# Macaron block with a state-space layer: B, C and dt in one projection, B stored four states side by side, clip and all products on GpSimd, new places in the order

## The chip, the cores and the metric

The kernel runs on one core of a Trainium2 chip. A core has five engines that run side by side and meet at semaphores: PE (TensorE, matmuls; PEld is its loading of weights), DVE (VectorE), ACT (ScalarE), POOL (GpSimd) and SP (SyncE, which issues nearly all DMAs here). The metric is the device time of one execution in microseconds; lower is better. The profile is one execution, read by a hardware profiler; an engine's "busy" time is the time in which at least one of its instructions ran.

## What is computed

The input x has 32 batches of 512 positions with 256 features. Three layers follow each other, each on the result of the one before: a feed-forward layer at half weight, a state-space layer, and the same feed-forward layer again.

```python
x = x + 0.5 * ffn(layernorm(x))
x = x + ssm(layernorm(x))
x = x + 0.5 * ffn(layernorm(x))
# ffn: every matmul's inputs are rounded to a grid of FP4 values in blocks of 16
h = silu(fp4(x) @ fp4(w_gate).T) * (fp4(x) @ fp4(w_up).T)      # 256 -> 704
y = fp4(h) @ fp4(w_down).T                                      # 704 -> 256
# ssm: N = 16 states for each of 256 features, R = 64
BC = x @ W_in + b_in;  B, C = BC[..., :16], BC[..., 16:]
dt = clip(softplus((x @ W_dt1 + b_dt1) @ W_dt2 + b_dt2), 1e-7, 1e6)
tmp = A * dt
h[t] = exp(tmp) * h[t-1] + expm1(tmp) / tmp * dt * B * x        # along the 512 positions
y = sum(h * C, over the states) + D * x
```

## The kernel before

**Order.** The kernel does not issue instructions where its loops stand. Its loops hand operations to a planner (`Plan.op`): engine, name, what is read, what is written. Each operation has a place in time, a number in the table `WHEN` under its name plus `PERIOD` for every batch. `Plan.run` then takes, again and again, among the operations whose inputs are ready and whose buffers are free in the plan, the one with the lowest number, and issues it. So the table sets the order on every engine's queue, the DMA queue of SP included; the hardware then runs each queue in that order and waits where it has to. The table is the same for all 32 batches. In the result several batches are under way at once: a batch's state-space layer runs beside feed-forward layers of its neighbours.

**Feed-forward** (`ffn`, L664). Layer norm (sums on DVE, four tiny operations on POOL, scaling on ACT), rounding to the grid (`quantize`, L527: the block's top, scale, reciprocal and quotient on DVE into the PSUM buffer `q`, square and curve on ACT, two matmuls with a large diagonal on PE that do the rounding, L563, a copy out on ACT, L569, and the product with the scale on POOL, L570), transposes on PE. Then four tiles of 128 positions: the "gate" and "up" matmuls (L676) in two halves of 352 columns, silu on ACT (L686), a copy of "up" on ACT (L696) and the product of both on POOL (L699); rounding; transposes (L710), copies (L715), the "down" matmuls (L722) and the sum (L729). One tile is different: in `(0, 0)`, the first tile of the first feed-forward layer, DVE multiplies straight out of PSUM (L692, "up silu") and neither the copy nor POOL's product is made.

**State-space layer** (`ssm`, L733). After layer norm and transposes, PE projects to B and C (L743, 32 columns) and, apart from that, to dt's 64 inner columns (L750). ACT adds the two biases (L745, L752). The 32 rows of B and C go to DRAM (L748). PE makes dt's 256 features in two halves (L757), ACT takes softplus (L761) in PSUM, DVE clips into SBUF (L764). Then for each half of the features (c) and each pair of states (NG = 2), 16 pairs in all: two rows of B and two of C come back from DRAM, spread to all 128 partitions (L780, L782, 512 KB each, two buffers each); ACT makes exp and tanh (L789, L792); POOL multiplies x with B, a pair at a time (L796); DVE makes, for each state, two products (L803, L806) and the scan along the positions (L809); POOL multiplies with C (L812); PE adds the states up while it turns them back (L818). A table load on ACT goes before each change between the function groups of silu, softplus and exp with tanh.

**Buffers.** PSUM: three of `pt` (projections, gates, transposes), one `q`, two `eb` (tanh to scan), one `py`.

Of the kernel before, what the change touches and what calls it, by code (L numbers as in the profile page):

```python
# [9 lines left out]
F32 = mybir.dt.float32  # L10
BF16 = mybir.dt.bfloat16
AF = mybir.ActivationFunctionType
# [19 lines left out]
        "weights load": (7249, 7248, 7249, 7249, 6726, 6726, 6642, 6642, 6642, 6841, 6841, 6841,  # L32
        6841),
        "weights x top": (7249, 7065, 7353),
        "weights x scale": (7250, 7248, 7385),
        "weights x rinv": (7250, 7248, 7391),
        "weights x quotient": (7250, 7248, 7391),
        "weights x square": (7250, 7249, 7392),
        "weights x curve": (7250, 7249, 7392),
        "weights x grid": (7250, 7249, 7557),  # L40
        "weights x rounded": (7250, 7249, 7557),
        "weights x value": (7250, 7249, 7558),
        "weights turn": (7251, 7251, 7249, 7249, 7558, 7558),
        "weights turned": (7251, 7251, 7250, 7251, 7558, 7558),
        "weights load down": (7065, 6579),
        "weights h top": (7558, 6642),
        "weights h scale": (7571, 6642),
        "weights h rinv": (7571, 6642),
        "weights h quotient": (7571, 6643),
        "weights h square": (7590, 6643),  # L50
        "weights h curve": (7590, 6643),
        "weights h grid": (7590, 6643),
        "weights h rounded": (7590, 6643),
        "weights h value": (7795, 7065),
        "weights turn down": (7795, 7795, 7699, 7661),
        "weights turned down": (7897, 7814, 8179, 7699),
        "weights zero rows": (8077, 8345),
        "in load": (0,),
        "ffn 0 stats": (1267, 1773, 601, 2361),
        "ffn 0 mean": (1913, 2355, 1536, 3584),  # L60
        "ffn 0 var + eps": (4038,),
        "ffn 0 rstd": (4045,),
        "ffn 0 - mean": (3609,),
        "ffn 0 shift": (4249,),
        "ffn 0 normal": (4499, 5056, 6579, 4467),
        "ffn 0 x top": (6643,),
        "ffn 0 x scale": (6726,),
        "ffn 0 x rinv": (6822,),
        "ffn 0 x quotient": (6835,),
        "ffn 0 x square": (6841,),  # L70
        "ffn 0 x curve": (6873,),
# [815 lines left out]
```

## Time and profile before

| | us |
|---|---|
| median of three runs | 3604.99 (3603.73 to 3605.07) |
| profiled execution, its own time | 3604.13 |
| profiled execution, span on the core | 3602.2 |
| DVE busy | 3409.9 |
| ACT busy | 3385.7 |
| PE busy | 3348.0 |
| POOL busy | 3332.3 |

The engines' shares are close to each other, so the page's totals alone do not say which of them sets the time. The stretch from the start to the first scan, the long repeating middle, and the stretch after the last scan have to be read apart, and in the middle the waits tell more than the busy shares. Numbers such as L796 are lines of the kernel file; "x512" is how often an instruction ran; after the bar stand the busy time, the mean of one, the idle time just before, and what ended it. DMA share is the mean busy share of 16 DMA engines.

### The profile page before, as it was taken

The page shows a single profiled execution, that of the slowest core. Times are in us where ns is not written, and L with a number is a line of the kernel's source. Part 1 is how long each engine was busy: PE and PEld are TensorE (multiplying, and loading weights), DVE is VectorE, ACT ScalarE, POOL GpSimd, SP SyncE. Part 2 cuts the span into 40 slices and gives each one's busy share as a digit, 9 for nine tenths or more (in the row PEclk, how much of TensorE's full clock was granted, in tenths as well). Part 3 has the DMA queues.
Part 4 walks back from the last instruction along what each step waited for, and adds up shares of the span by engine and source line. Part 5 has one row for each costly group of instructions (what it writes and reads, how often), then busy time and mean ns, then how long its engine had stood idle before and what let it go on. Part 6 is the DMA issues. An engine that isn't in the chain of part 4 may idle for free. (4 is left out here: it accounts for less than half of the span.)

```text
span 3602.2 us, 51333 instructions
## 1 busy us (share of the span) xinstructions
PE 3348.0 (93%) x16604; PEld 2443.6 (68%) x16826; DVE 3409.9 (95%) x5280; ACT 3385.7 (94%) x5813; POOL 3332.3 (93%) x1963
## 2 busy tenths in 40 slices
PE   5779999999999999999999999999999999999966
PEld 3457777667767767777766776776777776777654
DVE  3699999999999999999999999999999999999992
ACT  4689999999999999999999999999999999999973
POOL 2589999999999999999999999999999999999992
PEclk9899999999999999999999999999999999999988
DMA  1354545444545545454544454444555454445440
GB/s 45 112 173 166 173 164 176 165 169 165 176 171 170 165 158 175 170 173 164 177 165 169 165 176 170 170 165 159 176 171 173 163 177 165 168 161 169 171 170 12
DMA packets 186652, 578.36 MB, mean 161 GB/s; under 512 B 19664, under 2 KB 54032, under 8 KB 186384
## 3 DMA queue, kind: packets, MB, share of 16 engines
q1 hardware_dynamic: 184816, 574.89, 46.7%
q8 instruction: 133, 2.18, 0.2%
q14 instruction: 135, 1.11, 0.1%
q10 hardware_dynamic: 1568, 0.18, 0.0%
HBM read 556.12 MB, written 18.87 MB: 160 GB/s over the span
## 5 line engine op out<-in xcount | busy, mean ns | idle before, releaser
L676 PE MATMUL pt<-w_guT,xqT 128*128 128x352 f32 x4096 | 1317.4, 466 | 26.1 <-DVE dt L764 16.3
L812 POOL TENSOR_TENSOR hs<-hs,bc 128x1024 f32<-128x1024 f32 x512 | 1214.0, 2371 | 9.3 <-DVE hs L809 2.6
L809 DVE TENSOR_TENSOR_SCAN hs<-ab,eb 128x512 f32<-128x512 f32 x1024 | 1202.4, 1197 | 4.5
L796 POOL TENSOR_TENSOR bx<-xT,bc 128x1024 f32<-128x1024 f32 x512 | 1171.2, 2294 | 30.3 <-DVE eb L806 15.9
L676 PEld LDWEIGHTS pt<-w_guT,xqT 128*128 128x128 f32 x4096 | 753.3, 192 | 409.7 <-DVE dt L764 24.0
L792 ACT ACTIVATE eb<-dt,a_half 128x512 f32<-128x512 f32 x1024 | 708.1, 700 | 36.1 <-DVE hs L809 29.5
L806 DVE SCALAR_TENSOR_TENSOR eb<-eb,a_inv,bx 128x512 f32<-128x512 f32 x1024 | 734.9, 743 | 2.7
L722 PE MATMUL pt<-w_dT,hqT 128*128 128x256 f32 x3072 | 717.0, 383 | 14.8 <-ACT hqT L715 14.8
L789 ACT ACTIVATE ab<-dt,a_sb 128x512 f32<-128x512 f32 x1024 | 700.8, 727 | 1.5
L803 DVE SCALAR_TENSOR_TENSOR eb<-ab,eb 128x512 f32<-128x512 f32 x1024 | 684.5, 682 | 11.4 <-ACT eb L792 7.6
L722 PEld LDWEIGHTS pt<-w_dT,hqT 128*128 128x128 f32 x3072 | 580.1, 192 | 140.4 <-ACT hqT L715 32.9
L818 PE MATMUL py<-ident,hs 128*128 128x128 f32 x4096 | 536.1, 276 | 26.1 <-POOL hs L812 25.8
L818 PEld LDWEIGHTS py<-ident,hs 128*128 128x128 f32 x4096 | 469.4, 142 | 102.0 <-POOL hs L812 38.3
L570 POOL TENSOR_TENSOR h_q<-h_q,h_sc 128x704 f32<-128x704 f32 x258 | 360.3, 1397 | 53.2 <-ACT h_q L569 52.6
L699 POOL TENSOR_TENSOR h<-h,sl 128x704 f32<-128x704 f32 x224 | 379.0, 1692 | 27.4 <-ACT h L696 22.4
L544 DVE TENSOR_REDUCE q<-h 128x44 f32<-128x704 f32 x258 | 227.0, 880 | 68.6 <-POOL h L699 43.8
L710 PE MATMUL pt<-ident,h_q 128*128 128x128 f32 x1536 | 237.0, 278 | 41.2 <-ACT h L696 24.1
L563 PE MATMUL q<-h_m,eye 128*128 128x192 bf16 (+1 forms) x873 | 191.6, 305 | 70.9 <-ACT h_m L556 62.0
L710 PEld LDWEIGHTS pt<-ident,h_q 128*128 128x128 f32 x1536 | 180.5, 141 | 110.3 <-ACT h L696 51.8
L563 PEld LDWEIGHTS <-eye 128*128 128x128 bf16 x1300 | 125.2, 99 | 183.9 <-issue 106.8
L715 ACT COPY hqT<-pt 128x256 f32<-128x256 f32 (+1 forms) x512 | 233.9, 487 | 6.1 <-PE pt L710 5.7
L686 ACT ACTIVATE sl<-pt 128x352 f32<-128x352 f32 x512 | 222.5, 463 | 16.6 <-PE pt L676 13.8
(78 smaller groups left out, 4134.6 us busy)
## 6 DMA issues: line engine op xcount, KB each, us to landing
bc<-rows SPq DMA_DIRECT2D x1024, 512.0 KB, 4.1
x<-in_L_attn_x_dram SPq DMA_DIRECT2D x32, 512.0 KB, 5.2
out_dram<-x SPq DMA_DIRECT2D x32, 512.0 KB, 7.3
rows<-bc SPq DMA_DIRECT2D x32, 64.0 KB, 3.4
xn<-in_L_ffn_w_up_dram SPq DMA_DIRECT2D x6, 128.0 KB, 2.2
h<-in_L_ffn_w_down_dram SPq DMA_DIRECT2D x2, 352.0 KB, 3.4
xn<-in_L_ffn_w_gate_dram SPq DMA_DIRECT2D x5, 128.0 KB, 2.2
w_dt_sb<-in_L_attn_W_dt_dram ACTq DMA_DIRECT2D x2, 64.0 KB, 5.5
```

What stands on the lines that cost most here:

```text
L676: pe.matmul(to()[:, :HALF], lhsT=xqT()[:, c, j * P : (j + 1) * P], rhs=w_guT()[:, c, o : o + HALF], start=(c == 0), stop=(c == NC - 1),)
L699: op("POOL", "product", lambda sl=sl, h=h: g.tensor_tensor(h(), h(), sl(), ALU.mult), [h, sl], [h])
L710: pe.transpose(pt()[:, i * P : (i + 1) * P], hq()[:, kcol[k] : kcol[k] + P], ident)
L722: pe.matmul(po()[:, :DM], lhsT=hqT()[:, k, :], rhs=w_dT()[:, k, :], start=(k == 0), stop=False,)
L789: op("ACT", "exp", lambda c=c, i=i, k=k, ab=ab: s.activation(ab()[:, i, :], dt()[:, c, :], AF.Exp, scale=a_sb[:, c, k : k + 1]), [(dt, c)] ...
L792: op("ACT", "tanh", lambda c=c, i=i, k=k, eb=eb: s.activation(eb[i](), dt()[:, c, :], AF.Tanh, scale=a_half[:, c, k : k + 1]), [(dt, c)], ...
L796: op("POOL", "x b", lambda c=c, bx=bx, bn=bn: g.tensor_tensor(bx().rearrange("p n l -> p l n"), xT()[:, c, :].unsqueeze(2).to_broadcast([P ...
L803: op("DVE", "e", lambda i=i, ab=ab, eb=eb: v.scalar_tensor_tensor(eb[i](), ab()[:, i, :], 1.0, eb[i](), ALU.add, ALU.mult), [(ab, i), eb[i ...
L806: op("DVE", "e x b", lambda c=c, i=i, k=n + i, eb=eb, bx=bx: v.scalar_tensor_tensor(eb[i](), eb[i](), a_inv[:, c, k : k + 1], bx()[:, i, : ...
L809: op("DVE", "scan", lambda i=i, h=h, ab=ab, eb=eb: v.tensor_tensor_scan(h()[:, i, :], ab()[:, i, :], eb[i](), 0.0, ALU.mult, ALU.add), [(a ...
L812: op("POOL", "h c", lambda h=h, cn=cn: g.tensor_tensor(flat(h()), flat(h()), flat(cn()), ALU.mult), [h, cn], [h])
L818: pe.matmul(py()[:, j, :], lhsT=h()[:, i, j * P : (j + 1) * P], rhs=ident, is_transpose=True, start=False, stop=False, skip_group_check=True,)
```

## The change

- **One projection.** The weights of dt's inner columns, B and C stand side by side in one tile of 96 columns (`w_p_sb`); one projection and one bias instruction take the place of two. dt's second matmul reads rows 0 to 63 of the result.
- **B is turned.** PE transposes B's 16 rows (four transposes of 128 positions), ACT copies the result, and four DMAs write it to DRAM so that the four states of a group (XG = 4) stand side by side for each position. C's rows are written as before.
- **x times B by fours.** B is loaded for four states at once, 1 MB, and POOL's product runs over 256 positions by four states: as many instructions of as many elements, with B read in runs of four and x spread over four instead of two. The result is written as before with the positions of a state side by side. Two instructions make a group's four states, one for each half of the positions.
- **Clip on POOL.** Softplus writes SBUF, POOL clips in place.
- **All products on POOL.** Tile (0, 0) loses its special form: ACT copies "up", POOL multiplies.
- **Places.** `WHEN` has new numbers throughout, and the first, second, last but one and last batch have tables of their own. The output is stored in four pieces of 128 KB, each behind its tile, instead of one of 512 KB.

The diff, without the tables:

```diff
-    def __init__(self):
-        self.ops, self.slots = [], {}
+    def __init__(self, tables):
+        self.ops, self.slots, self.tables = [], {}, tables
...
-        o.at = (WHEN[o.name][k] + self.batch * PERIOD, len(self.ops))
+        table = self.tables.get(self.batch, WHEN)
+        o.at = (table[o.name][k] + self.batch * PERIOD, len(self.ops))
...
+    XG = 4
...
-    nc.scalar.dma_start(w_in_sb, w_in.rearrange("(c p) n -> p c n", p=P))
-    nc.scalar.dma_start(w_dt1_sb, w_dt1.rearrange("(c p) r -> p c r", p=P))
+    nc.scalar.dma_start(w_p_sb[:, :, R:], w_in.rearrange("(c p) n -> p c n", p=P))
+    nc.scalar.dma_start(w_p_sb[:, :, :R], w_dt1.rearrange("(c p) r -> p c r", p=P))
...
-    plan = Plan()
+    plan = Plan({0: FIRST, 1: SECOND, NB - 2: LAST_BUT_ONE, NB - 1: LAST})
...
-                if (which, j) in BY_DVE:
+                if (which, j) in PRODUCT_BY_DVE:
...
-        op("PE", "bc", lambda: project(pbc()[: 2 * N, :], w_in_sb), [xT], [pbc])
-        bc = new(sp, [2 * N, L], F32, "bc", 1)
-        op("ACT", "bc bias", lambda: s.activation(
-            bc(), pbc()[: 2 * N, :], AF.Identity, bias=b_in_sb), [pbc], [bc])
-        rows = new(dr, [2 * N, L], F32, "rows", 2)
-        op("SP", "rows", lambda: nc.sync.dma_start(rows(), bc()), [bc], [rows])
-        p1 = new(ps, [P, L], F32, "pt", PT)
-        op("PE", "dt1", lambda: project(p1()[:R, :], w_dt1_sb), [xT], [p1])
-        r1 = new(sp, [R, L], F32, "r1", 1)
-        op("ACT", "dt1 bias", lambda: s.activation(
-            r1(), p1()[:R, :], AF.Identity, bias=b_dt1_sb), [p1], [r1])
+        op("PE", "project", project, [xT], [pbc])
+        bc = new(sp, [R + 2 * N, L], F32, "bc", 1)
+        op("ACT", "project bias", lambda: s.activation(
+            bc(), pbc()[: R + 2 * N, :], AF.Identity, bias=b_p_sb), [pbc], [bc])
+        rows_c = new(dr, [N, L], F32, "rows_c", 2)
+        op("SP", "rows c", lambda: nc.sync.dma_start(rows_c(), bc()[R + N :, :]), [bc], [rows_c])
+        pb = new(ps, [P, L], F32, "pt", PT)
+
+        def turn_b():
+            for j in range(NJ):
+                pe.transpose(pb()[:, j * N : (j + 1) * N], bc()[R : R + N, j * P : (j + 1) * P],
+                             ident[R : R + N, R : R + N])
+
+        op("PE", "turn b", turn_b, [bc], [pb])
+        bT = new(sp, [P, NJ, N], F32, "bT", 2)
+        op("ACT", "turned b", lambda: s.copy(flat(bT()), pb()[:, : NJ * N]), [pb], [bT])
+        rows_b = new(dr, [N // XG, L, XG], F32, "rows_b", 2)
+
+        def side_by_side():
+            with nc.allow_non_contiguous_dma(reason="the states of a group side by side, 32 KB"):
+                for i in range(N // XG):
+                    nc.sync.dma_start(
+                        rows_b()[i].rearrange("(j p) n -> p j n", p=P),
+                        bT()[:, :, i * XG : (i + 1) * XG])
+
+        op("SP", "rows b", side_by_side, [bT], [rows_b])
...
-            op("DVE", "dt", lambda c=c: v.tensor_scalar(
-                dt()[:, c, :], p2[c](), 1e-7, 1e6, ALU.max, ALU.min), [p2[c]], [(dt, c)])
+            if CLIP_BY == "POOL":
+                op("ACT", "softplus", lambda c=c: s.activation(
+                    dt()[:, c, :], p2[c](), AF.Softplus, bias=b_dt2_sb[:, c : c + 1]),
+                   p2[c:], [(dt, c)])
+                op("POOL", "dt", lambda c=c: g.tensor_scalar(
+                    dt()[:, c, :], dt()[:, c, :], 1e6, 1e-7, ALU.min, ALU.max),
+                   [(dt, c)], [(dt, c)])
...
-                bn, cn = (new(st, [P, NG, L], F32, f"bc{i}", 2) for i in range(2))
-                op("SP", "load b", lambda n=n, bn=bn: nc.sync.dma_start(
-                    bn(), rows()[n : n + NG, :].partition_broadcast(P)), [rows], [bn])
+                if n % XG == 0:
+                    bn = new(st, [P, L, XG], F32, "bn", 2)
+                    bx = new(st, [P, XG, L], F32, "bx", 2)
+                    op("SP", "load b", lambda n=n, bn=bn: nc.sync.dma_start(
+                        bn(), rows_b()[n // XG].partition_broadcast(P)), [rows_b], [bn])
+                    for o in range(0, L, L * NG // XG):
+                        t = slice(o, o + L * NG // XG)
+                        op("POOL", "x b", lambda c=c, bx=bx, bn=bn, t=t: g.tensor_tensor(
+                            bx()[:, :, t].rearrange("p n l -> p l n"),
+                            xT()[:, c, t].unsqueeze(2).to_broadcast([P, L * NG // XG, XG]),
+                            bn()[:, t, :], ALU.mult), [(xT, c), bn], [(bx, o)])
+                cn = new(st, [P, NG, L], F32, "cn", 2)
...
-                bx = new(st, [P, NG, L], F32, "bx", 2)
-                op("POOL", "x b", lambda c=c, bx=bx, bn=bn: g.tensor_tensor(
-                    bx().rearrange("p n l -> p l n"),
-                    xT()[:, c, :].unsqueeze(2).to_broadcast([P, L, NG]),
-                    bn().rearrange("p n l -> p l n"), ALU.mult),
-                   [(xT, c), bn], [bx])
...
-        op("SP", "store", lambda b=b, x3=x3: nc.sync.dma_start(
-            out[b].rearrange("(j p) d -> p j d", p=P), x3()), [x3], [])
+        for j in range(NJ):
+            op("SP", "store", lambda b=b, j=j, x3=x3: nc.sync.dma_start(
+                out[b, j * P : (j + 1) * P, :], x3()[:, j, :]), [(x3, j)], [])
```

## The prediction

> **What bounds the kernel now.** I read the page's first part, the busy time in stretches, the waits in the repeating middle, the groups of instructions and the DMA issues, in that order. Overall, then in stretches (columns: stretch, its length, busy time and instruction count of PE, PEld, DVE, ACT, POOL, then PE's clock, DMA share, GB/s):
>
> ```profile
> PE 3348.0 (93%) x16604; PEld 2443.6 (68%) x16826; DVE 3409.9 (95%) x5280; ACT 3385.7 (94%) x5813; POOL 3332.3 (93%) x1963
> ```
>
> ```profile
> 0.00:132.00 132.00, 80.91 (x282) 48.90 (x286) 42.28 (x94) 63.77 (x100) 32.72 (x38) 0.92 0.16 50
> 132.00:200.00 68.00, 47.95 (x222) 36.07 (x223) 66.14 (x100) 53.73 (x91) 59.79 (x29) 0.85 0.50 174
> 200.00:300.00 100.00, 87.03 (x414) 61.45 (x418) 96.25 (x149) 91.74 (x153) 92.04 (x55) 0.97 0.48 164
> 300.00:3300.00 3000.00, 2896.90 (x14588) 2125.19 (x14784) 2981.89 (x4615) 2959.18 (x5105) 2927.00 (x1722) 1.00 0.49 169
> ...
> 3400.00:3517.50 117.50, 81.97 (x393) 59.86 (x397) 110.77 (x152) 89.10 (x144) 104.48 (x54) 0.84 0.48 166
> 3517.50:3602.20 84.70, 56.01 (x217) 39.01 (x217) 14.88 (x29) 30.82 (x55) 19.17 (x15) 0.84 0.04 13
> ```
>
> From 300 to 3300 us DVE is busy 99.4%, ACT 98.6%, POOL 97.6%, PE 96.6%. The run loses its time in the first 132 us (before the first scan) and the last 85 (after the last one). The middle repeats exactly: the one DMA per batch that writes the rows of B and C (timeline of SP) goes out at
>
> ```profile
> 1068.48 0.42 SPq L748 DMA_DIRECT2D rows<-bc  x1
> ...
> 2877.46 0.42 SPq L748 DMA_DIRECT2D rows<-bc  x1
> ```
>
> 17 batches apart, so (2877.46 - 1068.48) / 17 = 106.41 us a batch. Waits between 1000 and 2000 us: DVE has none at all, ACT these:
>
> ```profile
> ACT x L729 <- PE pt L726: 2.6, 9, 0.3
> ACT xn_s L522 <- POOL shift L519: 1.9, 9, 0.2
> ACT eb L792 <- DVE hs L809: 1.8, 9, 0.2
> ```
>
> That is 6.3 us in 1000, 0.67 us a batch. So DVE is the bound and ACT is second by only 0.67 us: without waits it would need 106.41 - 0.67 = 105.74 us. This decides the case: taking work off DVE is worth at most what ACT lets through.
>
> The rows that price the change:
>
> ```profile
> L796 POOL TENSOR_TENSOR bx<-xT,bc 128x1024 f32<-128x1024 f32 x512 | 1171.2, 2294 | 30.3 <-DVE eb L806 15.9
> L699 POOL TENSOR_TENSOR h<-h,sl 128x704 f32<-128x704 f32 x224 | 379.0, 1692 | 27.4 <-ACT h L696 22.4 <-issue 2.7 <-DVE h_sc L546 1.6
> L570 POOL TENSOR_TENSOR h_q<-h_q,h_sc 128x704 f32<-128x704 f32 x258 | 360.3, 1397 | 53.2 <-ACT h_q L569 52.6 <-DVE eb L806 0.4
> L570 POOL TENSOR_TENSOR x_q<-x_q,x_sc 128x1024 f32<-128x1024 f32 x67 | 129.7, 1936 | 60.5 <-ACT x_q L569 60.5
> L692 DVE TENSOR_TENSOR h<-pt,sl 128x352 f32<-128x352 f32 x64 | 32.8, 512 | 13.3 <-PE pt L676 10.2
> L764 DVE TENSOR_SCALAR dt<-pt 128x512 f32<-128x512 f32 x64 | 40.4, 671 | 14.9 <-ACT pt L761 14.9
> L696 ACT COPY h<-pt 128x352 f32<-128x352 f32 x448 | 191.2, 450 | 7.9 <-PE pt L676 7.6
> L745 ACT ACTIVATE bc<-pt,b_in_sb 32x512 f32<-32x512 f32 x32 | 21.2, 664 | 1.2 <-PE pt L741 1.2
> ```
>
> ```profile
> bc<-rows SPq DMA_DIRECT2D x1024, 512.0 KB, 4.1
> out_dram<-x SPq DMA_DIRECT2D x32, 512.0 KB, 7.3
> rows<-bc SPq DMA_DIRECT2D x32, 64.0 KB, 3.4
> d_sb<-in_L_attn_D_dram ACTq DMA_DIRECT2D x1, 1.0 KB, 2.1
> ```
>
> **DVE** loses the product of tile 0 (32.8 us) and the clip (40.4): -73.2, or 2.3 us a batch; its floor falls to 104.1.
>
> **ACT** gains 64 copies of "up" at 191.2 / 448 = 0.427: +27.3. Two bias instructions become one (rows of 512 elements whatever the partitions): -21.2. One new copy per batch of 64 elements: the copies of 512 and 256 elements take 596 and 378 ns, so 64 come to 215: +6.8. Softplus writes SBUF instead of PSUM; exp (to SBUF, 727 ns) against tanh (to PSUM, 700) gives 0 to +1.7, I take +0.9. Table loads by the new order: 286 against 284, at 1.283: +2.6, none of it in the middle (9 a batch in both). Sum +16.4; in the middle 0.43 a batch, so ACT's floor becomes 105.74 + 0.43 = 106.17. ACT is the new bound, and the repeating middle can gain only 0.24 us a batch.
>
> **POOL** gains 32 products at 1.692: +54.1. The 64 clips (512 elements, in place) are not in the trace. Above: the two value rows give (1936 - 1397) / 320 = 1.68 ns an element, so 1.07 us. Below: GpSimd's memsets of 1 and 128 elements (98 and 204 ns) extrapolate to 0.53. I take the middle, 0.80, as a clip lies between them (one read, one write): +51 (34 to 69). The x-times-B product keeps its count (512 of 1024 elements) but now spreads each x over four products, reads B in runs of four, and writes with the old stride. Below: the value product, whose second input is spread over 16, 1936 ns. Above: 2294, no gain; I exclude a loss, since the writes are strided as before and the reads less so. I take 2.05, nearer the value row: -125 (0 to -183). The clip waits on POOL for softplus, and behind it stand an h-times-C and the batch's first x-times-B; DVE, which waited there before, had one wait of note, 14.9 us in the head. POOL in all 3332.3 + 54.1 + 51 - 125 = 3312 (3237 to 3455): its load hardly changes, 0.6 us a batch less.
>
> [...]
>
> **PE** loses one of two projections (60.9 us for the 32-column one) and gains 128 transposes of 16 columns, between 0.1 us (a weight load alone, 109 ns) and 0.28 (a transpose of 128): +13 to +35. All beside other work.
>
> **DMA and SP.** B comes in 256 loads of 1 MB for 512 of 512 KB, the same bytes. New are four small DMAs a batch, 512 pieces of 16 bytes each, between the turned B and the first load of B. Let X be their time to landing, all four. Below: 2.1 us (the D vector, 256 pieces of 4 bytes). Above: the output store, 512 pieces of 1 KB, 7.3, then three more at 5.2: 22.9. I take 8: as many pieces as the store, 1/64 of its bytes. What hides X: in the new order ACT runs 19.3 us of work (by the rows' durations, softplus and three table loads included) from the turned B to the first exp of that batch, and about 4 us more pass to the first e-times-B on DVE: 23. The chain beside it: four issues at 0.35, X, a 1 MB load (4.1 for half; 6), two halves of x-times-B (4.2): 11.6 + X. So it is covered up to X = 11.4. Queued on SP behind the wait for the turned B are one piece of the output, one load of C for the batch before, and the first two loads of B; POOL waits for them. [...]
>
> **Places.** ACT idles 216.5 us before: 68.2 up to 132 us, 22.5 up to 300, 40.8 + 2.7 up to 3400, 28.4 up to 3517.5, and 53.9 after.
> - Middle: 19.5 us of the idle are waits, the rest gaps of some nanoseconds between instructions. Behind a DVE that is now 2 us ahead I take two thirds of the waits away: -13 (0 to -19.5; new waits are a rival).
> - 132 to 300 and 3400 to 3517.5: DVE is busy 273.2 of 285.5 us, it bounds there, and 2.1% of its work is gone: -6.
> - Head: the bias of B and C is reached after the same instructions of PE as before, in another order: the last matmuls of "gate" and "up" now stand before tile 2's rounding, where four used to stand after it. In DVE's timeline the tops of the four tiles start at 62.7, 69.3, 78.5 and 91.5 us, and one weight block waits 10.3 us at 46: against an even 6.6 a tile that is 2.6 + 6.4 + 10.3, some 19 us that an order could save; I take 12. The longer path of B (X - 3.4, a longer load, a second half of the product: about 9) is partly covered by 18 "gate" and "up" matmuls of the next batch moved beside it; I take 4. So -8 (from +9 to -19).
> - Tail: after the last scan stand the same four tiles in both; the last copy ends 3.9 us before the end, and the store behind it shrinks from 512 to 128 KB: -2. Order within: -2 (+5 to -6).
>
> **Sum**, against the profiled execution: 3602.2 + 16.4 - 13 - 6 - 8 - 4 = 3587.6, plus 1.9 around the span (3604.13 - 3602.2) = 3589.5. The median of the runs is 0.9 above that execution: 3590.
>
> **Rivals.**
> 1. POOL becomes the bound: slower. POOL needs 103.8 us a batch now, plus about 0.6 of gaps. It decides when 103.8 + 1.7 + 1.6 - 16 d exceeds 105.6, d being what one x-times-B gains: from d under 0.095 us, a product above 2.20 us. With no gain and the dear clip, 107.6 + 0.6 = 108.2 a batch: +1.8 x 31 = 56, about 3650 with the rest of the sum. For it: the strided writes stay. Against: both rows with a widely spread input are below 2 ns an element.
> 2. The small DMAs land late: X above 11.4 stalls POOL, then DVE, then ACT once a batch. X = 13 gives 1.6 x 31 = +50: 3640. For it: 2048 pieces a batch. Against: the D vector's 2.1 us.
> 3. The new order couples worse: with buffers as few (two for e, one for q, three for pt), ACT waits up to 1 us a batch more rather than 0.42 less: up to 1.42 x 31 = 44, 3605 to 3634. For it: ACT and POOL share more hand-overs (product, clip) than DVE did. Against: ACT's waits of 0.67 are few though it is within 0.7% of the bound already.
> 4. Better than forecast: no waits of ACT in the middle, all 19 us of the head: 3602.2 + 16.4 - 19.5 - 6 - 19 - 6 + 2.8 = 3571.
>
> **How the numbers follow.** Forecast 0.45 (its own range 3574 to 3605: 0.36 faster, 0.09 about the same); rival 4 0.17; rival 3 0.16 (0.07 same, 0.09 slower); rival 1 0.10; rival 2 0.12. 0.2% is 7.2 us, about what a measurement of this kernel can tell from no change. Faster 0.53, same 0.16, slower 0.31. The range takes rival 4 and most of 3, and reaches to the near ends of 1 and 2: 3562 to 3640.
>
> **What would show it.** Right: ACT 99% or more of the middle with waits near nothing, DVE near 98%; the period 106.1 to 106.4; x-times-B near 2.05 us; the clip near 0.8. Wrong: POOL waiting for the loads of B once a batch (rival 2), POOL's share of the middle above 99% (rival 1), ACT's waits above 1 us a batch (rival 3), a first scan later than 136 us (the head).

## The result: slower by 0.9%, and the profile after

The changed kernel takes 3635.33 us, median of four runs (3633.61 to 3643.2), against 3604.82 before: a ratio of 1.0089, 95% interval [1.0072, 1.0107]. The profiled execution took 3633.61 us with a span of 3631.8, 29.6 us longer than the span before.

The first line of the page after, and the busy time in stretches (columns as in the prediction):

```profile
PE 3337.3 (92%) x16605; PEld 2463.0 (68%) x16826; DVE 3405.7 (94%) x5152; ACT 3415.4 (94%) x5879; POOL 3294.1 (91%) x2059
```

```profile
0.00:132.00 132.00, 88.87 (x325) 55.80 (x330) 55.48 (x110) 80.51 (x131) 48.74 (x48) 0.95 0.23 67
...
300.00:3300.00 3000.00, 2854.37 (x14367) 2111.50 (x14561) 2931.36 (x4443) 2943.78 (x5090) 2853.92 (x1781) 0.99 0.52 167
```

No engine is full any more in the middle: DVE is busy 97.7%, ACT 98.1%, PE and POOL 95.1%. The time that DVE, PE and POOL were relieved of has become idle time. PE's clock, 1.00 before, is 0.99.

The rows that priced the change:

```profile
L1739 POOL TENSOR_TENSOR bx<-xT,bn 128x1024 f32<-128x1024 f32 x512 | 1038.1, 2039 | 15.6 <-DMA bn<-rows_b 9.4 <-DVE eb L1762 5.3
L1710 POOL TENSOR_SCALAR dt<-dt 128x512 f32<-128x512 f32 x64 | 39.2, 613 | 6.7 <-ACT dt L1707 2.2
L1688 ACT COPY bT<-pt 128x64 f32<-128x64 f32 x32 | 6.4, 198 | 0.9 <-PE pt L1683 0.8
L1675 ACT ACTIVATE bc<-pt,b_p_sb 96x512 f32<-96x512 f32 x32 | 21.5, 672 | 3.0 <-PE pt L1670 3.0
```

x-times-B took 2.04 us (2.05 forecast), the clip 0.61 (0.80), the copy of the turned B 0.198 (0.215). So the loss is not in the price of a part; it is in when things run. I mark each batch by ACT's copy of the second "y" (L834 before, L1790 after). In ACT's timeline, first before, then after:

```profile
664.98 0.60 ACT L834 COPY x<-py 128x512 f32<-128x512 f32 x1
771.39 0.60 ACT L834 COPY x<-py 128x512 f32<-128x512 f32 x1
877.79 0.60 ACT L834 COPY x<-py 128x512 f32<-128x512 f32 x1
```

```profile
668.90 0.60 ACT L1790 COPY x<-py 128x512 f32<-128x512 f32 x1
777.47 0.59 ACT L1790 COPY x<-py 128x512 f32<-128x512 f32 x1
884.20 0.60 ACT L1790 COPY x<-py 128x512 f32<-128x512 f32 x1
992.75 0.60 ACT L1790 COPY x<-py 128x512 f32<-128x512 f32 x1
1099.48 0.60 ACT L1790 COPY x<-py 128x512 f32<-128x512 f32 x1
```

Before, every middle period is 106.41 within 0.02. After, these four are 108.57, 106.73, 108.55 and 106.73: a short period, and one that is 1.8 us longer, by turns; the other batches lie at or between these two values. From batch 4 to batch 28 the mean is (3254.16 - 668.90) / 24 = 107.72. By these marks the 29.6 us are:

| stretch | before | after | difference |
|---|---|---|---|
| start to the mark of batch 0 | 238.46 | 227.60 | -10.9 |
| batch 0 to 3 (the loop fills) | 320.10 | 334.43 | +14.3 |
| batch 3 to 28 | 2660.29 | 2692.13 | +31.8 |
| batch 28 to the end | 383.35 | 377.64 | -5.7 |

Both ends come out shorter, as forecast, but the head's gain does not last: the first scan starts 15.2 us earlier (at 120.7 us for 135.9), the mark of batch 0 comes 10.9 us earlier, that of batch 3 comes 3.5 us later. The middle, forecast at -13, loses 32. Of these, 25 x (106.75 - 106.41) = 8.5 us lie in the short period itself; the rest, 23, in the long ones.

**What the long periods have in common** came out only after the first experiments, but it is read from this trace. PE's timeline at the turned B, in a short period (first lines) and in a long one; the bracket is the idle time before the instruction and what ended it:

```profile
1066.90 1.04 PE L1774 MATMUL py<-ident,hs 128*128 128x128 f32 x8
1068.28 0.66 PE L1512 MATMUL pt<-ident,x_q 128*128 128x128 f32 x4 [0.35 <-POOL x_q L1499]
1068.87 0.42 PE L1683 MATMUL pt<-ident,bc 16*128 16x16 f32 x4
1070.01 0.66 PE L1512 MATMUL pt<-ident,x_q 128*128 128x128 f32 x4 [0.72 <-ACT bT L1688]
1070.59 1.98 PE L1702 MATMUL pt<-bc,w_dt_sb 64*128 64x512 f32 x4
...
959.75 0.66 PE L1512 MATMUL pt<-ident,x_q 128*128 128x128 f32 x4 [0.34 <-POOL x_q L1499]
960.34 0.42 PE L1683 MATMUL pt<-ident,bc 16*128 16x16 f32 x4
961.47 0.66 PE L1512 MATMUL pt<-ident,x_q 128*128 128x128 f32 x4 [0.72 <-ACT bT L1688]
962.06 3.38 PE L1702 MATMUL pt<-bc,w_dt_sb 64*128 64x512 f32 x4
```

The same four matmuls of dt take 1.98 us in one batch and 3.38 in the other. The busy time says why, in two stretches of 7 us each, at the same place of the long batch (first lines) and of the short one (the sixth value is PE's granted clock, after the five engines' busy times):

```profile
955.00:962.00 7.00, 5.57 (x30) 3.08 (x29) 6.93 (x14) 6.85 (x13) 6.18 (x4) 1.00 0.23 75
962.00:969.00 7.00, 7.00 (x23) 4.50 (x22) 6.55 (x9) 6.36 (x10) 5.28 (x3) 0.54 0.46 34
...
1063.53:1070.53 7.00, 5.59 (x30) 3.10 (x29) 6.93 (x14) 6.85 (x13) 6.20 (x4) 1.00 0.22 75
1070.53:1077.53 7.00, 6.39 (x32) 3.84 (x31) 6.77 (x9) 6.94 (x12) 5.25 (x3) 1.00 0.62 43
```

In the long batch the clock is at half right behind the place where PE waits 0.34 us for x_q, does four transposes of 16 columns, and waits 0.72 us for ACT's copy of the turned B. Up to there PE does the same in both batches (busy 5.57 and 5.59 us). What differs is the moment: in the clock record of this trace all 68 entries, each at half or in full, begin on one grid of 3.41 us (within 0.01 us), and a batch of 106.7 us is 31.3 of its steps, no whole number, so the place lies differently in the grid from batch to batch. Read in steps of half a microsecond, the middle of the changed kernel (300 to 3300 us) has 15 such falls; 13 of them start 78 to 80 us after a mark, which is this place. Eight of the 13 last 6.8 us, and their periods are 108.53 to 108.57; five last 3.4 us, and theirs are 106.85 to 108.12. The kernel before has none between 252 and 3414 us. ACT's timeline shows how a fall reaches the others: its copy of h_q comes late, waiting for PE's rounding.

```profile
969.88 0.74 ACT L1498 COPY h_q<-q 128x704 f32<-128x704 f32 x1 [1.46 <-PE q L1487]
```

The batches with a fall in batches 4 to 27 stand 17.5 us above the short period in sum, the others 5.7. Of the others, eight are more than 0.15 us above it, and in seven of these POOL waits for a load of C or of B some 90 us after the mark. The longest is batch 18 with 108.19 us (timelines of SP and POOL):

```profile
2252.89 2.02 SPq L1694 DMA_DIRECT2D rows_b<-bT  x4
2255.55 0.38 SPq L1744 DMA_DIRECT2D cn<-rows_c  x1
...
2265.45 2.35 POOL L1768 TENSOR_TENSOR hs<-hs,cn 128x1024 f32<-128x1024 f32 x1 [1.60 <-DMA cn<-rows_c]
```

This load of C stands on SP's queue behind the wait for the turned B and the four small DMAs; it landed 9.7 us after it went out, where the median is 4.1.

In the kernel before, PE has no gap at this place. There the second projection stood, the 1.9 us that the change took away:

```profile
1062.78 1.93 PE L741 MATMUL pt<-xT,w_dt_sb 128*64 128x512 f32 x4
1064.64 1.90 PE L741 MATMUL pt<-xT,w_in_sb 128*32 128x512 f32 x4
1066.47 0.66 PE L583 MATMUL pt<-ident,x_q 128*128 128x128 f32 x4
1067.06 1.12 PE L757 MATMUL pt<-r,w_dt_sb 64*128 64x512 f32 x2
```

Gaps alone do not make a fall, though. Once a batch, at another place, the kernel before has a longer pair of gaps, and its clock stays at 1.00 (PE's timeline, then the busy time of the stretch):

```profile
1633.97 0.76 PE L563 MATMUL q<-h_m,eye 128*128 128x512 bf16 x4 [0.97 <-ACT h_m L556]
1635.15 0.66 PE L710 MATMUL pt<-ident,h_q 128*128 128x128 f32 x4 [0.42 <-ACT h L696]
...
1632.90:1636.30 3.40, 2.00 (x16) 1.42 (x14) 3.40 (x5) 3.40 (x8) 3.40 (x2) 1.00 0.49 169
```

PE is busy for 2.00 us of this step of the grid; in the steps ahead of the 13 falls it is busy for 2.34 to 2.70. What the place of the falls has besides its gaps is matmuls on few rows (the first number of "16*128"): B's transposes use 16, dt's four matmuls, which stand together there, 64; the matmuls around them use 128. As an estimate from the traces, weigh PE's time by the rows used, out of 128: the steps ahead of the 13 falls then come to 44 to 54% of full, and no step of the kernel before between 300 and 3196 us is under 59%. But six other steps of the changed kernel lie between 44 and 54%, and two, in batches 0 and 1, at 43%, without a fall. So the rows may be part of it; no run here changes them alone, and what exactly brings a fall stays open.

The clock record of this trace holds 0.5 and 1.0 only, and the same program falls in some batches and not in others: two gaps of 0.35 and 0.72 us with four tiny matmuls between them are followed by a fall in about half of the 28 batches that pass this place between 300 and 3300 us.

### The profile page after: what moved, and what is told of

It is laid out like the page before. It is cut to its first block, busy times and chain, and to the rows that moved or that the text cites. A ratio compares the mean times of both kernels' runs of the same rounds, so it can differ in the third digit from the quotient of the medians.

```text
span 3631.8 us, 51218 instructions
## 1 busy us (share of the span) xinstructions
PE 3337.3 (92%) x16605; PEld 2463.0 (68%) x16826; DVE 3405.7 (94%) x5152; ACT 3415.4 (94%) x5879; POOL 3294.1 (91%) x2059
## 4 chain that ended last, share of the span: by engine, by line
PE 36%; ACT 26%; DVE 16%; POOL 10%; issue 5%; DMA 5%; SPq 0%; ACTq 0%; DVEq 0%; POOLq 0%
PE pt L1605 16%; PE pt L1651 6%; ACT ab L1751 5%; DVE hs L1765 5%; PE py L1774 5%; ACT eb L1754 4%; POOL bx L1739 4%; POOL hs L1768 4%; DMA bn<-rows_b 3%; PE q L1487 3%; DVE eb L1762 3%; DVE eb L1759 2%; PE pt L1639 2%; DVE q L1474 2%; ACT h_m L1480 2%
## 5 line engine op out<-in xcount | busy, mean ns | idle before, releaser
L1768 POOL TENSOR_TENSOR hs<-hs,cn 128x1024 f32<-128x1024 f32 x512 | 1210.4, 2365 | 91.1 <-PE py L1774 22.5
L1765 DVE TENSOR_TENSOR_SCAN hs<-ab,eb 128x512 f32<-128x512 f32 x1024 | 1209.4, 1205 | 23.9 <-PE py L1774 13.3
L1739 POOL TENSOR_TENSOR bx<-xT,bn 128x1024 f32<-128x1024 f32 x512 | 1038.1, 2039 | 15.6 <-DMA bn<-rows_b 9.4
L1762 DVE SCALAR_TENSOR_TENSOR eb<-eb,a_inv,bx 128x512 f32<-128x512 f32 x1024 | 747.1, 747 | 30.8 <-POOL bx L1739 15.2
L1751 ACT ACTIVATE ab<-dt,a_sb 128x512 f32<-128x512 f32 x1024 | 712.9, 728 | 1.7 <-DVE hs L1765 0.2
L1651 PEld LDWEIGHTS pt<-w_dT,hqT 128*128 128x128 f32 x3072 | 572.7, 192 | 99.8 <-ACT hqT L1644 16.0
L1774 PE MATMUL py<-ident,hs 128*128 128x128 f32 x4096 | 544.6, 284 | 39.5 <-POOL hs L1768 39.5
L1774 PEld LDWEIGHTS py<-ident,hs 128*128 128x128 f32 x4096 | 489.9, 147 | 126.7 <-issue 57.9
L1628 POOL TENSOR_TENSOR h<-h,sl 128x704 f32<-128x704 f32 x256 | 430.9, 1683 | 52.6 <-ACT h L1625 41.6
```

The lines of the kernel that those rows point to most:

```text
L1628: op("POOL", "product", lambda sl=sl, h=h: g.tensor_tensor(h(), h(), sl(), ALU.mult), [h, sl], [h])
L1651: pe.matmul(po()[:, :DM], lhsT=hqT()[:, k, :], rhs=w_dT()[:, k, :], start=(k == 0), stop=False,)
L1739: op("POOL", "x b", lambda c=c, bx=bx, bn=bn, t=t: g.tensor_tensor(bx()[:, :, t].rearrange("p n l -> p l n"), xT()[:, c, t].unsqueeze(2).t ...
L1751: op("ACT", "exp", lambda c=c, i=i, k=k, ab=ab: s.activation(ab()[:, i, :], dt()[:, c, :], AF.Exp, scale=a_sb[:, c, k : k + 1]), [(dt, c)] ...
L1762: op("DVE", "e x b", lambda c=c, i=i, k=n + i, eb=eb, bx=bx: v.scalar_tensor_tensor(eb[i](), eb[i](), a_inv[:, c, k : k + 1], bx()[:, k % ...
L1765: op("DVE", "scan", lambda i=i, h=h, ab=ab, eb=eb: v.tensor_tensor_scan(h()[:, i, :], ab()[:, i, :], eb[i](), 0.0, ALU.mult, ALU.add), [(a ...
```

## The experiments

**First: order or parts?** My first theory was that the new order couples worse, whatever the parts; the rival was that the parts themselves cost it.

Run 1, the parts of the kernel before in the places of the changed kernel (four buffers instead of two for B and for x-times-B, so that this order can be issued):

```diff
-PERIOD = 3379; WHEN = {... before's places ...}
+PERIOD = 3379; WHEN = {... each operation at its rank in the changed kernel's order ...}
-    bn, cn = (new(st, [P, NG, L], F32, f"bc{i}", 2) for i in range(2))
+    bn, cn = (new(st, [P, NG, L], F32, f"bc{i}", [4, 2][i]) for i in range(2))
-    bx = new(st, [P, NG, L], F32, "bx", 2)
+    bx = new(st, [P, NG, L], F32, "bx", 4)
```

> The parts of the kernel before (two projections, B by pairs from plain rows, clip and one product on DVE), but every operation in the rank that it has in the changed kernel's issue order; four buffers for pairs of B and of x times B, so that they can run as far ahead as there. Theory 'order': the 1.3 us a batch that the middle lost comes from the new places, whatever the parts; then the middle takes 107 to 108.5 us a batch here and the time is 3620 to 3660. Rival 'parts': the loss comes from the longer path of B (small DMAs, 1 MB loads) and the hand-overs to POOL; then the middle is back at 106.4 and the time is 3575 to 3605.

3982.64 us, 1.1047 [1.103, 1.1063].

Run 2, all new parts in the places of the kernel before (new operations put directly behind the ones they take their input from):

```diff
-plan = Plan({0: FIRST, 1: SECOND, NB - 2: LAST_BUT_ONE, NB - 1: LAST})
+plan = Plan({})    # WHEN: before's one table under the new names
```

> All parts of the change, but the one table of places of the kernel before for all batches; a new operation takes the place of the one it replaces, the two halves of x times B the place of the first pair's product. 'Order': the middle takes 106.1 to 106.6 us a batch, 3590 to 3612. 'Parts': the middle stays at 107.5 or more, 3635 to 3660.

4017.47 us, 1.1145 [1.1126, 1.1163]. Here DVE waits for POOL's product of tile (0, 0), 108.1 us in eight waits between 1000 and 2000 us, 13.5 us a batch, since nobody had made room for it on POOL:

```profile
DVE q L545 <- POOL h L705: 108.1, 8, 13.7
```

Run 3, the changed kernel with clip and product back on DVE, in the new places:

```diff
-CLIP_BY = "POOL"
-PRODUCT_BY_DVE = set()
+CLIP_BY = "DVE"
+PRODUCT_BY_DVE = {(0, 0)}
```

> The changed kernel with its places, but the clip and the product of tile 0 of the first layer back on DVE. 'Order': the time stays within 12 us of 3635. 'Parts', by the hand-overs ACT to POOL alone: 3600 to 3620. If DVE is again the bound with its 73 us: above 3640.

3921.24 us, 1.0878 [1.0862, 1.0895]. That is above 3640, but the loss of 286 us is four times the 73 us that went back to DVE, so DVE as the bound does not explain it either.

Run 4, the kernel before with the new order only in its first two batches and its last two (the edit in words; it is a table of places):

```diff
-    sequence = before
+    sequence = first 1132 operations by the changed kernel's order + before's middle + the rest by the changed kernel's order
```

> The parts of the kernel before and its order, except that what it issues up to the third batch's projection, and from the end of batch 29's state-space layer on, stands in the changed kernel's rank (buffers of B and x times B as in the first run). The traces put the ends of the changed kernel 10.9 us (to the end of the first batch's state-space layer) and 12.9 us (after the last) ahead. 'Ends gain by order': 3575 to 3595. Rival 'the ends' gain is only work put off to the next batches, or needs the new parts': 3598 to 3612.

3611.08 us, 1.0019 [1.001, 1.0029]. The shorter head and tail of the changed kernel do not come with the order alone.

Neither theory holds. Parts and order each cost 9 to 11% without the other, ten times the change's own effect, so these runs say nothing about its 0.9%. PE's clock was lower in the first three (0.947, 0.945 and 0.939 on the mean, against 0.984 before and 0.974 after), a sign that I passed over at this point.

**Second: take a little work from one engine at a time.** This asks which engine is the bound, with every engine's order kept.

```diff
 # run 5: DVE
-op("DVE", "e", lambda i=i, ab=ab, eb=eb: v.scalar_tensor_tensor(
+op("DVE", "e", lambda c=c, k=n + i, i=i, ab=ab, eb=eb: (c, k) not in ((0, 8), (0, 9)) and v.scalar_tensor_tensor(
 # run 6: ACT
-op("ACT", f"{tag} curve", lambda: s.activation(
+op("ACT", f"{tag} curve", lambda: what not in ((0, 1), (1, 1)) and s.activation(
 # run 7: POOL
-    dt()[:, c, :], dt()[:, c, :], 1e6, 1e-7, ALU.min, ALU.max),
+    dt()[:, c, :16], dt()[:, c, :16], 1e6, 1e-7, ALU.min, ALU.max),
 # run 8: PE
-pe.matmul(po()[:, :DM], lhsT=ident, rhs=src()[:, j, :], start=False, stop=True)
+if (which, j) not in ((0, 1), (0, 2)):
+    pe.matmul(po()[:, :DM], lhsT=ident, rhs=src()[:, j, :], start=False, stop=True)
```

> The changed kernel, every engine's order kept, with DVE's product e left out for two of the 32 state rows of a batch (states 8 and 9 of the first half of the features; tanh goes on as it is): 2 x 0.683 = 1.37 us a batch less for DVE, 44 us in all. Theory 'loop' (in the middle no engine is the bound, a round of hand-overs through all of them is): a part comes back, 5 to 20 us: 3615 to 3630. Rival 'bound by DVE': 35 to 44 us: 3591 to 3600. Rival 'bound by ACT' (98.1% busy): nothing, 3630 to 3638.

> The changed kernel, every engine's order kept, with ACT's 'curve' of the rounding left out for tile 1 of both feed-forward layers: 2 x 0.789 = 1.58 us a batch less for ACT, 50 us in all. Theory 'loop': 10 to 25 us come back: 3610 to 3625. Rival 'bound by ACT': 40 to 50: 3585 to 3595. Rival 'bound by DVE': nothing.

> The changed kernel, every engine's order and every hand-over kept, with POOL's clip cut from 512 to 16 columns (the other columns of dt are not clipped): from 0.613 to about 0.1 us each, 1.0 us a batch, 33 us in all. Theory 'loop': 3 to 15 us come back: 3620 to 3632. Rivals 'bound by DVE' or 'by ACT': nothing, 3630 to 3638.

> The changed kernel, every engine's order kept, with the matmul that adds the input (L1655) left out for tiles 1 and 2 of the first feed-forward layer, so these two tiles lack the residual: 152.4 / 256 = 0.60 us a tile, 1.2 us a batch less for PE, 38 us in all. Theory 'loop': 8 to 25 us come back, since PE has the largest share (36%) of the chain that ended last: 3610 to 3627. Rivals 'bound by DVE' or 'by ACT': nothing, as PE is busy 95% only: 3630 to 3638.

Run 9 takes away the waits on the way of B:

```diff
-for i in range(N // XG):                       # the four small DMAs
+for i in range(0):
-bn(), rows_b()[n // XG].partition_broadcast(P)
+bn(), x[b, 2 * n : 2 * n + 8, :].rearrange("a (l n) -> (a l) n", n=XG).partition_broadcast(P)
```

> The changed kernel with the four small DMAs left out and the loads of B reading the input instead (8 rows of it, as large, to as many partitions; so B's values are wrong); orders kept otherwise. SP no longer waits for the turned B, and no load waits for rows in DRAM. Theory 'loop': the way of B is one edge of the round and seldom the last (POOL waits only 6 us of 3000 for a load of B): 0 to 12 us come back: 3623 to 3635. Rival 'B's longer way sets the round' (11.3 us for the first load, once a batch, in the chain that ended last): the whole loss of the middle, 25 to 32 us: 3603 to 3610.

| run | work taken away, us in all | time | ratio to before | against 3635.33 | usual short period | falls, 300 to 3300 us |
|---|---|---|---|---|---|---|
| changed kernel | - | 3635.33 | 1.0089 [1.0072, 1.0107] | - | 106.73 to 106.88 | 15 |
| 5, DVE | 44 | 3626.69 | 1.0062 [1.0047, 1.0077] | -8.6 | 106.74 to 106.87 | 13 |
| 6, ACT | 50 | 3624.93 | 1.0065 [1.0048, 1.0082] | -10.4 | 106.58 to 106.82 | 10 |
| 7, POOL | 64 x (0.613 - 0.199) = 26 | 3628.34 | 1.0067 [1.0052, 1.0082] | -7.0 | 106.73 to 106.77 | 10 |
| 8, PE | 38 | 3624.92 | 1.0063 [1.0047, 1.008] | -10.4 | 106.75 to 106.89 | 8 |
| 9, B's rows ready | the waits for them | 3623.40 | 1.0055 [1.004, 1.007] | -11.9 | 106.72 to 106.86 | 12 |

(The falls and periods are those of the one profiled execution.) The times fit 'loop': no cut returns more than a third of itself. The intervals of runs 5 to 8 overlap that of the changed kernel, so each of these gains is at the edge of what can be told; run 9's is clear of it. But the periods tell something else. The short period does not move at all, except by 0.15 us for ACT; all five runs gain about the same, and what differs is how many periods are long. That is what led to the clock.

Run 9 also prices the longer way of B. The short period is the same, so that way has no part in it. But the long batches without a fall are gone: such batches stand 0.6 us above the short period in sum, against 5.7 in the changed kernel, and with them go POOL's waits for loads between 300 and 3300 us (the changed kernel, then run 9, where no wait for a load of B is left):

```profile
POOL hs L1768 <- DMA cn<-rows_c: 14.3, 15, 3.3
POOL bx L1739 <- DMA bn<-rows_b: 6.0, 10, 1.5
...
POOL hs L1768 <- DMA cn<-rows_c: 1.5, 2, 1.1
```

So the small DMAs are not wholly covered, as the forecast had them: by this estimate they cost some 5 us in all, mostly through the loads of C behind them.

The same cuts in the kernel before:

```diff
 # run 11: DVE
+op("DVE", "e", lambda c=c, k=n + i, i=i, ab=ab, eb=eb: (c, k) not in ((0, 8), (0, 9)) and v.scalar_tensor_tensor(
 # run 12: ACT
+op("ACT", f"{tag} curve", lambda: what not in ((0, 1), (1, 1)) and s.activation(
 # run 18: PE
+if (which, j) not in ((0, 1), (0, 2)):
```

> The kernel before, every engine's order kept, with DVE's product e left out for the same two state rows: 1.37 us a batch less. The prediction's reading (DVE bounds, ACT is second by 0.67 us a batch): 0.67 x 30 = 20 us and a little at the ends: 3575 to 3587. Rival 'loop, before too': 5 to 12 us or a loss: 3593 to 3610. Rival 'DVE alone': 3561 to 3568.

> The kernel before, every engine's order kept, with ACT's 'curve' left out for tile 1 of both feed-forward layers: 1.58 us a batch less for ACT, 50 us in all. The prediction's reading (DVE bounds): nothing in the middle, 0 to 6 us at the ends: 3599 to 3605. Rival 'loop, before too': 10 to 25 us: 3580 to 3595.

> The kernel before, every engine's order kept, with the matmul that adds the input left out for tiles 1 and 2 of the first feed-forward layer (these tiles lack the residual): 1.2 us a batch less for PE, 38 us in all, at places where PE is dense. Rival 'PE bounds the kernel before' (96.6% busy; cutting DVE gave nothing): 3565 to 3572. Theory 'loop': 3594 to 3606, and no falls of the clock, as the gap is not beside others.

Run 11: 3607.31 us, 1.0008 [0.9999, 1.0018]; run 12: 3599.07, 0.9984 [0.9975, 0.9994]; run 18: 3602.28, 0.9996 [0.9987, 1.0006]. So 44 us less for DVE, busy 99.4% of the middle, give nothing; most of its time turns into waits, which were not there before (between 1000 and 2000 us):

```profile
DVE q L544 <- ACT x_q L569: 6.0, 10, 0.9
DVE eb L803 <- ACT eb L792: 3.7, 10, 0.4
```

The periods are 106.41 to 106.44 (three at 106.8) for DVE, 106.24 for ACT, 106.39 for PE. Run 12 misses the range of 'loop' and lies at the edge of the other one, which expected nothing in the middle; 0.17 us a batch came back there. None of these three engines sets the period by itself. What does set 106.41 is not settled: POOL was not cut there, and a round of hand-overs whose members were not among the cut operations would look the same. There are no falls of the clock in the middle of these three.

Run 10, the clip alone on DVE, in SBUF:

```diff
-op("POOL", "dt", lambda c=c: g.tensor_scalar(
+op("DVE", "dt", lambda c=c: v.tensor_scalar(
```

> The changed kernel with the clip alone handed to DVE, in place in SBUF after softplus as POOL does it (so the PSUM buffer is not held for it); product and all places as changed. It splits the run in which clip and product both went to DVE and which took 3921 us. If the loss there was the PSUM buffer held until DVE's clip (41 us of PE waits in 1000): little here, 3630 to 3680. If it was the placing of DVE's extra work: 3700 to 3850.

3732.61 us, 1.0359 [1.0343, 1.0374]: without the PSUM buffer held, a clip that DVE reaches late still costs 97 us. ACT waits for it at its first exp:

```profile
POOL h L1628 <- DVE eb L1759: 32.8, 9, 4.5
...
ACT ab L1751 <- DVE dt L1710: 25.0, 9, 3.6
```

The period grows by 110.64 - 107.72 = 2.9 us, close to the 2.8 a batch that ACT waits here; PE's clock falls 35 times in this run's middle, too, and the two are not told apart. In this order the clip is better off on POOL.

**Third: is it the clock?** Run 13 fills PE's wait with a dead matmul, run 14 with a third of it, run 15 (the control) puts one elsewhere, and run 16 shortens the wait by moving ACT's copy one instruction up.

```diff
 # runs 13 and 14, at the end of turn_b: n = 384 and n = 128
+pe.matmul(pb()[:, 64 : 64 + n], lhsT=ident, rhs=xT()[:, 0, :n], start=True, stop=True)
 # run 15, behind "down" of tile (0, 1)
+pe.matmul(po()[:, DM : DM + 256], lhsT=ident, rhs=w_guT()[:, 0, :256], start=True, stop=True)
 # run 16, ACT's order in batches 3 to 29
-... tanh, exp, exp, copy of the turned B, ...
+... tanh, exp, copy of the turned B, exp, ...
```

> The changed kernel, every engine's order kept, with one matmul of 384 columns more on PE behind the four small transposes of B, into columns of the same buffer that nobody reads; it lies in PE's wait of 0.7 us for ACT's copy of the turned B. Theory 'clock': that wait and the wait before it let TensorE's clock fall to half for 3.4 us at a time (15 times between 300 and 3300 us, each from 78 to 80 us after the batch's second y, none in the kernel before), and each fall lengthens its batch by 1.8 us. Filled, the falls go and every middle period is 106.75: about 26 us back, 3605 to 3612. Rival 'loop, whatever the clock': the time stays or grows by PE's 0.6 us a batch, 3633 to 3645.

> As the run with the wait filled, but with a matmul of 128 columns, a third as long (about 0.2 us of the 0.7). Theory 'clock': fewer falls than 15, not none: 3608 to 3630. Rival 'loop': 3633 to 3640.

> The control: the changed kernel with one matmul of 256 columns more per batch where PE is dense (behind 'down' of tile 1 of the first feed-forward layer, into columns that nobody reads). Theory 'clock': the falls after the turned B stay, 10 to 16 of them, and the time stays at 3633 to 3642.

> The changed kernel with ACT's copy of the turned B moved ahead of the one exp that stands before it (27 batches; all other orders kept). PE's wait for the copy shrinks from 0.72 to about 0.2 us. Theory 'clock': the falls of the clock go or nearly so, middle periods near 106.75: 3603 to 3615. Rival 'loop': within 5 us of 3635.

| run | time | ratio to before | falls, 300 to 3300 us | usual short period | mean, batch 4 to 28 |
|---|---|---|---|---|---|
| changed kernel | 3635.33 | 1.0089 [1.0072, 1.0107] | 15 | 106.73 to 106.88 | 107.72 |
| 13, 384 columns | 3631.03 | 1.0073 [1.0056, 1.0089] | 1 | 107.21 to 107.25 | 107.44 |
| 14, 128 columns | 3620.38 | 1.0046 [1.0031, 1.0061] | 2 | 106.79 to 106.83 | 107.11 |
| 15, elsewhere | 3633.19 | 1.0078 [1.0063, 1.0093] | 11 | 106.78 to 106.82 | 107.43 |
| 16, copy earlier | 3636.81 | 1.009 [1.0075, 1.0106] | 15 | 106.96 to 107.03 | 107.71 |

Run 13 does what the theory says to the clock: no fall is left after batch 1. It misses in time, since the dead matmul does not only fill the wait. It writes the buffer that ACT's copy reads, so the copy waits for it too (ACT's timeline):

```profile
1072.00 0.21 ACT L1689 COPY bT<-pt 128x64 f32<-128x64 f32 x1 [0.30 <-PE pt L1685]
```

and the short period grows by 0.5 us. Run 14 ends soon enough that ACT does not wait, leaves the short period within 0.05 us, and 15 us come back: half of what the change had lost, for more work on PE. The two intervals, up to 1.0061 here and from 1.0072 for the changed kernel, do not meet. The control keeps 9 falls at the place, one fewer than expected, in the fastest of its four executions; its interval, from 1.0063, does not meet run 14's either. Run 16 misses, with the time of the rival: the wait for the copy shrank, but a wait for the copy of xqT, now behind it, took its place (PE's timeline):

```profile
961.90 0.66 PE L7928 MATMUL pt<-ident,x_q 128*128 128x128 f32 x4 [0.34 <-POOL x_q L7915]
962.48 0.42 PE L8099 MATMUL pt<-ident,bc 16*128 16x16 f32 x4
963.20 0.65 PE L7928 MATMUL pt<-ident,x_q 128*128 128x128 f32 x4 [0.30 <-ACT bT L8104]
964.30 1.98 PE L8118 MATMUL pt<-bc,w_dt_sb 64*128 64x512 f32 x4 [0.44 <-ACT xqT L7931]
```

0.34 + 0.30 + 0.44 = 1.08 us of gaps against 0.35 + 0.72 = 1.07, and 15 falls as before. The run did not take away what it was to take away, so it decides nothing between the two.

**Last: one part alone.** Run 17 is the kernel before with one projection instead of two, at the place of dt's, every order kept:

```diff
-op("PE", "bc", lambda: project(pbc()[: 2 * N, :], w_in_sb), [xT], [pbc])
-project(p1()[:R, :], w_dt1_sb)
+project(p1()[: R + 2 * N, :], w_p_sb)
-r1(), p1()[:R, :], AF.Identity, bias=b_dt1_sb
+r1(), p1()[: R + 2 * N, :], AF.Identity, bias=b_p_sb
-nc.sync.dma_start(rows(), bc())
+nc.sync.dma_start(rows(), r1()[R:, :])
```

> One part of the change alone: the kernel before, every engine's order kept, with B, C and dt's inner columns in one projection at the place of dt's (the second projection and the bias of B and C are left out; rows of B and C go to DRAM from the same buffer). PE loses 1.9 us a batch (60.9 us in all), ACT 0.66 (21 us), at the place where the changed kernel's clock falls and where the kernel before has no gap. Theory 'clock and loop': the freed PE time becomes a gap there, and where it is long enough the clock falls, 1.7 us each: 3600 to 3630, with falls in some batches. Rival 'work': less work is faster, 3584 to 3602, no falls.

3604.75 us, 1.0004 [0.9994, 1.0013]. 61 us of PE and 21 us of ACT are gone and nothing is gained: the period is 106.40, and PE's time has become a wait at that very place.

```profile
1063.11 1.88 PE L739 MATMUL pt<-xT,w_p_sb 128*96 128x512 f32 x4
1066.11 0.66 PE L581 MATMUL pt<-ident,x_q 128*128 128x128 f32 x4 [1.12 <-POOL x_q L568]
1066.70 1.12 PE L754 MATMUL pt<-r,w_dt_sb 64*128 64x512 f32 x2
```

One batch of 32 has a fall in the middle, and its period is 107.99. So the gap opens with the one projection, but by itself and with dense work around it it came with one fall in the middle; in the changed kernel the turned B with its tiny matmuls and its wait comes on top, and dt's four matmuls stand together.

No version here that does all the work beats the kernel before; run 12, 0.16% faster, leaves some out.

## Why the prediction was wrong

The range (3562 to 3640) held the time by luck: its upper end stood for the near ends of rivals 1 and 2, and neither is what mainly happened. The sign was wrong. By its own steps:

- **"So DVE is the bound and ACT is second by only 0.67 us"** is the step that failed. I read 99.4% busy and no waits as a bound. Run 11 took 1.37 us a batch from DVE and the usual period stayed within 0.03 us of 106.41; run 12 took 1.58 from ACT and it fell by 0.17; PE gave 0.02. Busy shares of 96 to 99% on four engines said that all were nearly full, not which one sets the pace. With that step fall the middle's gain (-13) and the -6 of the stretches where DVE is busiest, and "ACT is the new bound": ACT ended at 98.1%, and 50 us less of it gave 10 at most.
- **"Middle: two thirds of the waits away".** ACT's waits between 1000 and 2000 us are about what they were, 6.7 us against 6.3. The loss is elsewhere: +31.8 us, of which 8.5 are the short period (106.75 for 106.41) and 23 the long ones. Runs 13 to 15 show that falls of PE's clock make most of the long ones: without nearly all of them, 15 us come back. I had seen the column of the clock, 1.00 in the middle, and taken it for granted.
- **PE loses 60.9 us and gains 13 to 35, "All beside other work".** The price was right (13.3 us of transposes) and the word "beside" was the trap. I priced the PE time that went at nothing and never asked what PE would do in its place: it waits there, 0.35 and 0.72 us a batch, and in about half the batches of the middle its clock falls right behind. In run 14, with 128 more columns of PE work at that place, the middle has 2 falls for 15.
- **Rival 3, "the new order couples worse"**, came nearest: 3605 to 3634, just under the 3635.33, for three `pt` buffers among others, and PE does now wait for a `pt` buffer at the turned B. But its sign (ACT's waits above 1 us a batch) did not appear; ACT waits 0.7.
- **Rival 1 is out, rival 2 came true in a small part.** POOL is busy 95.1% of the middle with x-times-B at 2.04 us. It waits 6.0 us in 3000 for loads of B, ten times, not once a batch, but 14.3 us for loads of C queued behind the small DMAs. Run 9, without these DMAs, has the same short period and some 5 us less in long batches without a fall.
- **Prices.** x-times-B, product, bias (672 ns on 96 partitions; before, 664 on 32 and 693 on 64), copies within 10%; the clip 0.61 for 0.80, within its bounds; POOL 3294 for 3312. ACT's busy time rose by 29.7 for 16.4. The durations of its instructions add up to only 9.5 us more; but consecutive instructions overlap a little in the traces, and after the change, with ACT idle for 56 us of the middle instead of 41, they do so less (475 us in all, 495 before). In the same way DVE's durations add up to 61 us less and its busy time to 4.2 less: they overlap for 347 us instead of 404.
- **Head -8, tail -4.** Measured by the marks, -10.9 and -5.7, but these stretches also hold those of the -6, and the head's gain is gone by batch 3; run 4 did not get it by the order alone. That the numbers are near is in part luck. Not in the sum at all: the loop takes 14.3 us more from batch 0 to batch 3 (periods 115.1, 111.3 and 108.0 for 107.3, 106.4 and 106.4). Run 9 shaves 2.7 us off that, so B's longer way explains little of it; three falls lie in these batches, against one before, and the rest stays open, as do the 8.5 us of the short period.

## What to carry to other kernels

Where four engines are each 95 to 99% busy, the busiest one is a guess (here DVE, at 99.4%: 44 us less for it in run 11 gave nothing back): before counting on its freed time, take a little work from it, order unchanged, and see whether the period moves. Work taken from PE was not free in the changed kernel, where it left gaps of 0.35 and 0.72 us: look at the granted clock just behind such a place, period by period, because the mean over the middle (0.99) hid a half clock in about every second batch. And compare periods, not totals: two clean values 1.8 us apart said more than any share of busy time.

## What I had not expected

- At gaps of 0.35 and 0.72 us, with four small transposes between them, the clock fell to half for 3.4 or 6.8 us in about half the batches; gaps of 0.97 and 0.42 us in the kernel before never did that, and a single gap of 1.12 us with dense work behind it (run 17) did so once in the middle.
- More PE work made the kernel faster: 128 dead columns a batch, 15 us.
- An order and the parts it was made for are one thing: exchanging either cost 9 to 11%, and moving the clips, two of 0.6 us a batch, to DVE's queue 97 us.
- The kernel before repeats its period within 0.02 us; four different cuts of 1.2 to 1.9 us a batch (runs 11, 12, 17 and 18) moved the usual period by 0.17 at most.
